# Leaving the order behind the attention to the scheduler, and issuing a batch's experts whole

## Chip, core and metric

The kernel runs on one core of one Trainium2 chip. The metric is the device time of one execution in microseconds (us), lower is better. A profiled execution of its own gives the span from the first to the last instruction and the trace.

## What is computed

One hybrid layer on x, of 4 batches x 1024 tokens x 128 features in fp32:

```python
x = x + softmax_attention(layernorm(x))        # 16 heads of 64, causal
x = x + experts(layernorm(x))                  # 32 experts 128x128, top 2 by softmax
x = x + linear_attention(layernorm(x))         # 16 heads of 8, cumulative sums over tokens
x = x + experts(layernorm(x))                  # the same experts again
```

`experts` multiplies each token with its two best experts' matrices, weighted with the softmax values. The linear attention forms `kv_cum = cumsum(k[:, :, None] * v[:, None, :])` over the tokens of a batch and divides `q . kv_cum` by `q . cumsum(k)`; the cumulative sums start anew with each batch.

## The kernel before

The tokens are held in SBUF in one tile, `x_sb`, as 32 tiles of 128 tokens, 8 to a batch. The kernel has three stages.

**Attention** (to L837) goes over 4 batches x 8 pairs of heads. The first `experts` of batches 0 to 2 are stepped beside it. It ends with the output projection of the last batch (`project_out`, L711 and L716), beside which the last gathers of batch 2 and the first statistics for the experts of batch 3 already run.

**Linear attention** goes over 32 steps u, one for each tile of 128 tokens. `prepare(t)` (L959 to L1034) makes the features of four tiles: statistics (L965), scaling (L980), transposes (L987), one product with all four weights (L998), four copies on ACT (L1002 to L1005), the bias on POOL (L1007), exponential, sigmoid and logarithm on ACT, and four sums on POOL (L1027, L1028). `products(u)` multiplies k and v into `kv` on POOL (L1048) and copies k on ACT (L1054). `cumulate(u)` adds kv to the running sums in PSUM with a triangular matrix on PE (L1066), `outputs(u)` multiplies them with q on DVE (L1086), `carry(u)` completes the sums for the next tile on PE (L1074), and `finish(u)` reduces, divides, transposes (L1107), projects (L1112) and adds to x_sb (L1115).

**Experts** (`experts`, L206 to L474) is a generator: each `yield` ends a step, and the caller decides what other work is issued between two steps. It has four parts:

1. Routing (L218 to L348): statistics, transposes and router products, softmax, top two, counts of tokens per expert (a matmul into `pc`, L290 and L294), and from the counts the row that each token has in a list sorted by experts. Work passes between DVE, POOL, ACT and PE some twenty times.
2. Scatter: 16 weighted tiles are made on ACT (L376) and written to `xs_d` in HBM by 16 indirect DMAs that POOL issues (L366), with a one-column memset (`between`, L370) behind each.
3. The loop over 47 blocks of 128 rows, in 12 groups: load of the rows (L402) and of the weights (L407; for the last 15 blocks SP loads the expert's number into a register, L411, and then issues a DMA of its own, L414), transposes (L433), copy (L435), products (L422), copy (L427), and store to `ys_d` (L428). All loads and stores stand in SP's queue.
4. Gather: 16 indirect DMAs on POOL (L441). For the first experts they add into x_sb; for the second ones (called with `came`) they land in tiles `y` that DVE adds (L468, L473), and the batch is written out (L474).

The second experts of batch 3 are done otherwise: `moe` (L850 to L928) multiplies its 8 tiles with all 32 experts: 128 matmul records at L900 (two to a matmul), whose results DVE (L915) and ACT (L908) weight and POOL sums (L922 to L924).

**The order.** From the attention's first instruction to the end of the linear attention, everything is within `order.enter_context(tc.manual_schedule())`: each engine takes its instructions in the order in which the program issues them, and that order is written out by hand. In the linear attention, `ahead(third)` is called three times a step; each call steps every running `prepare` once and then calls `beside()`, which pops one entry of `queue` (one scatter or one gather), starts a waiting batch's experts if its room is free, and steps each running `experts` once:

```python
        def beside():
            if queue:
                queue.pop(0)()
            while waiting and not rooms[(waiting[0] + 1) % 2].busy:
                b = waiting.pop(0)
                r = rooms[(b + 1) % 2]
                sides.append(experts(b, f"s{b}", banks, queue, r, came))
            for e in list(sides):
                if next(e, "end") == "end":
                    sides.remove(e)
```

So the first experts of batch 3 ("3") run beside the linear attention of batches 0 and 1, the second experts of batch b ("s0", "s1", "s2") are put on the waiting list at step u = 8b + 11, and what is left of s1 and s2 goes on beside `moe`, which lies behind `order.close()`.

PSUM tiles of the linear attention and of the experts come from one pool of four banks (`ps_l`, tag `ps1`); the running sums (`ps_c`) and the reduced outputs (`ps_n`) have banks of their own. The divided outputs `o` have three buffers, `m` two, `kv` three.

Of the kernel before, what the change touches and what calls it, by code (L numbers as in the profile page):

```python
# [20 lines left out]
def hybrid_kernel(  # L21
# [455 lines left out]
    order = ExitStack()  # L477
    order.enter_context(tc.manual_schedule())
    sides, queue = [], []
    banks = [None]  # L480
    with attn as ph:
# [253 lines left out]
        def beside(k):  # L735

            for _ in range(3 if k % 2 else 1):
# [5 lines that stand above are left out]
# [10 lines left out]
        def slot(u, two, k):  # L753
# [36 lines left out]
            next(outs, None)  # L790
            next(norms, None)
            beside(k)
            if u3 and u3.ib % 2:
                weighing.append(weigh(*units[-4][1]))
# [36 lines left out]
        for _ in project_out(*pend):  # L831
            if k == 1:
                assert not room.busy
                sides.append(experts(B - 1, f"{B - 1}", banks, queue, room))
                final = sides[-1]
            beside(k)
            k += 1  # L837

    late = ctx.enter_context(tc.tile_pool(name="late", bufs=1, reuse_waits="tile"))
    xp = ctx.enter_context(tc.tile_pool(name="xp", bufs=1, reuse_waits="tile"))
# [7 lines left out]
    def moe(nm_, store, first=0, beside=None, between=None):  # L850
        with ExitStack() as ph:
# [4 lines left out]
            for q in range(first, NT // 4):  # L856
                nm = f"{nm_}_{q}"
                c0 = q * 4
                if beside:
                    beside(q, ps_1)  # L860
# [175 lines left out]
    with lin as ph:  # L1036
# [86 lines left out]
# [5 lines that stand above are left out]
                b = waiting.pop(0)  # L1128
                r = rooms[(b + 1) % 2]
                sides.append(experts(b, f"s{b}", banks, queue, r, came))  # L1130
            for e in list(sides):
                if next(e, "end") == "end":
                    sides.remove(e)

        def ahead(third):

            nonlocal started
            while started < NT // G and 3 * G * started - AHEAD <= third:
                if G * started // NB == B - 1 and final in sides:
                    break  # L1140
                running.append(prepare(started, ps_1))
                started += 1
            for r in list(running):
                if next(r, "end") == "end":
                    running.remove(r)
            beside()

        for third in range(-AHEAD, 0):
            ahead(third)
        kv = products(0)  # L1150
        ends = []
        for u in range(NT + 4):
# [18 lines left out]
                ends.append(f)  # L1171
                kv = nkv
            ahead(3 * u + 2)
    order.close()

    def rest(pool):

# [40 lines left out]
```

## Time and profile before

| | before |
|---|---|
| median of 3 runs | 2079.35 us (2077.35 to 2085.32) |
| profiled execution, its own time | 2080.02 us |
| span of the profiled execution | 2078.1 us |
| granted TensorE clock, mean | 0.938 |
| last gather of the first experts of batch 2 issued (end of the attention's part) | 1502.4 us |
| first scatter of "3" / first load of its loop / its first gather | 1568.0 / 1617.0 / 1670.8 us |
| first scatter of s0 / first load of its loop / its first gather | 1782.7 / 1825.6 / 1896.5 us |
| last addition of the linear attention to x_sb (L1115) | 1891.3 us |
| last gather of s2 | 2049.7 us |

Busy time by stretches of the span, in us; the last two columns are the granted clock of TensorE and the mean busy share of the DMA engines:

| stretch | length | PE | DVE | ACT | POOL | clock | DMA |
|---|---|---|---|---|---|---|---|
| 0 to 1504, attention | 1504 | 1427.41 | 1069.24 | 979.81 | 830.54 | 0.99 | 0.12 |
| 1671 to 1727 | 56 | 38.42 | 32.03 | 26.57 | 47.23 | 0.85 | 0.15 |
| 1825 to 1892 | 67 | 49.87 | 36.45 | 19.40 | 33.04 | 0.75 | 0.53 |
| 1957 to 2028 | 71 | 54.57 | 35.01 | 18.20 | 27.72 | 0.78 | 0.60 |

An engine's row in the profile gives its line in the source, the engine, the operation, and "output<-inputs" by the program's names. SPq and POOLq are the queues of SP and of POOL: what they issue or wait for. Times in a timeline are a start and a duration, both in us; "[1.42 <-DVE m]" is idle time of the engine ahead of an instruction and what ended it. PE's durations are modelled.

### The profile page before, as it was taken

To read this page: it belongs to the slowest core of one execution; us is meant where nothing else is said; L and a number is where in the kernel's file an instruction comes from. 1 tells how busy PE (TensorE), PEld (TensorE's weight loads), DVE (VectorE), ACT (ScalarE), POOL (GpSimd) and SP (SyncE) were. 2 spreads that over 40 slices of the span, in tenths; PEclk is the share of its full clock that TensorE was granted. 3 is DMA by queue.
4 is the path that set the end of the run, shared out by engine and by line. 5 is a ranking of instruction groups with operands and counts; after the bars stand their busy time and mean duration, and the time that the engine had idled before them with its cause. 6 is when DMAs were issued, how large, how long until landed. Compare 5 with 4: busy or idle time off the path is not lost. (4 is left out here: it accounts for less than half of the span.)

```text
span 2078.1 us, 33646 instructions
## 1 busy us (share of the span) xinstructions
PE 1816.7 (87%) x10117; PEld 1056.7 (51%) x10117; DVE 1368.5 (66%) x3983; ACT 1200.5 (58%) x3721; POOL 1203.1 (58%) x2216
## 2 busy tenths in 40 slices
PE   5999999999999999999999999999547767774776
PEld 2555555555555655555565555556323534453442
DVE  4677776776887677678767777776326457653545
ACT  3766666676676566667756676676264444422322
POOL 3444444454675486466547645663748477966735
PEclk9999999999999999999999999999868988885877
DMA  7000000000003210000331000033300510054751
GB/s 209 1 1 1 1 1 1 1 1 1 1 16 102 83 17 5 1 1 12 91 95 19 8 1 1 12 87 98 67 0 18 163 33 7 20 162 124 205 152 37
DMA packets 173059, 96.56 MB, mean 46 GB/s; under 512 B 9264, under 2 KB 170064, under 8 KB 172752
## 3 DMA queue, kind: packets, MB, share of 16 engines
q1 hardware_dynamic: 158256, 78.16, 13.3%
q0 software_dynamic: 14336, 14.69, 3.3%
q8 instruction: 82, 1.34, 0.3%
q10 hardware_dynamic: 288, 1.57, 0.2%
q14 instruction: 97, 0.79, 0.1%
HBM read 57.23 MB, written 37.16 MB: 45 GB/s over the span
## 5 line engine op out<-in xcount | busy, mean ns | idle before, releaser
L599 DVE TENSOR_REDUCE nmx<-s 128x2 f32<-128x1024 f32 x512 | 604.2, 1219 | 217.5 <-PE s L590 207.2
L624 ACT ACTIVATE p<-s,nmx 128x512 f32<-128x512 f32 (+3 forms) x640 | 361.2, 575 | 316.3 <-DVE nmx L599 261.7
L590 PE MATMUL s<-kT,qT 64*128 64x512 f32 x2048 | 516.6, 618 | 8.5 <-ACT p L624 4.7
L666 POOL TENSOR_SCALAR p<-p,f,ri 128x512 f32<-128x512 f32 (+3 forms) x768 | 504.7, 675 | 0.7 <-DVE x_sb L716 0.2
L679 PEld LDWEIGHTS pt<-ident,p 128*128 128x128 f32 x2304 | 250.7, 141 | 218.8 <-issue 101.2
L679 PE MATMUL pt<-ident,p 128*128 128x128 f32 x2304 | 336.4, 282 | 25.3 <-ACT pT L683 7.6
L683 ACT COPY pT<-pt 128x512 f32<-128x512 f32 (+3 forms) x768 | 324.7, 509 | 14.9 <-PE pt L679 9.3
L648 POOL TENSOR_TENSOR rs<-rs,f 128x2 f32<-128x2 f32 x256 | 52.5, 205 | 428.0 <-ACT f L615 388.6
L696 PE MATMUL po<-pT,va 128*64 128x256 f32 (+1 forms) x2560 | 291.2, 365 | 0.6 <-DVE oT L703 0.6
L590 PEld LDWEIGHTS s<-kT,qT 64*128 64x128 f32 x2048 | 173.3, 185 | 194.6 <-issue 96.2
L629 ACT ACTIVATE p<-s,nmx 128x128 f32<-128x128 f32 x512 | 180.6, 366 | 103.4 <-DVE nmx L599 93.4
L696 PEld LDWEIGHTS po<-pT,va 128*64 128x64 f32 x2560 | 167.1, 136 | 97.2 <-issue 32.6
L644 POOL TENSOR_TENSOR rs<-rs 128x2 f32<-128x2 f32 x192 | 44.0, 229 | 193.7 <-DVE ri L657 193.7
L637 DVE SCALAR_TENSOR_TENSOR p<-p,qtri 128x128 f32<-128x128 f32 x512 | 145.3, 310 | 7.1 <-ACT p L629 4.0
L624 ACT ACTIVATION_READ_ACCUMULATOR p<-s,nmx 128x1 f32 x640 | 138.9, 217 | 0.0
L441 POOL DMA_INDIRECT x_sb<-ys_d,row x64 | 102.6, 1604 | 16.5 <-issue 16.4
L1066 PE MATMUL cum<-kv,tri 128*128 128x384 f32 x192 | 78.3, 549 | 27.0 <-POOL kv L1048 23.1
L716 DVE TENSOR_TENSOR x_sb<-pw,x_sb 128x128 f32<-128x128 f32 x128 | 36.9, 288 | 79.4 <-PE pw L711 78.2
L711 PE MATMUL pw<-wo_sb,oT 128*128 128x128 f32 x512 | 84.5, 290 | 0.7
L900 PE MATMUL pe_s<-we_sb,xnT_ms 128*128 128x512 f32 x128 | 75.0, 716 | 9.9 <-DVE x_sb L915 7.2
L711 PEld LDWEIGHTS pw<-wo_sb,oT 128*128 128x128 f32 x512 | 68.6, 190 | 27.9 <-ACT pT L683 12.7
L422 PE MATMUL pe_s<-we_s,xsT_s 128*128 128x128 f32 x282 | 53.3, 330 | 32.9 <-issue 19.1
(300 smaller groups left out, 2684.5 us busy)
## 6 DMA issues: line engine op xcount, KB each, us to landing
xs<-xs_d SPq DMA_DIRECT2D x44, 256.0 KB
ys_d<-ys SPq DMA_DIRECT2D x44, 256.0 KB
xs_s<-xs_d SPq DMA_DIRECT2D x33, 256.0 KB
ys_d<-ys_s SPq DMA_DIRECT2D x33, 256.0 KB
we<-_ffn_expert_weights_dram SPq DMA_DIRECT2D x32, 256.0 KB
we_s<-_ffn_expert_weights_dram SPq DMA_DIRECT2D x24, 256.0 KB
xs_d<-zero SPq DMA_DIRECT2D x2, 3008.0 KB
we<-_ffn_expert_weights_dram SPq DMA_DIRECT2D x60, 64.0 KB
```

The source lines that it names most:

```text
L441: g_.indirect_dma_start(to, None, yd, bass.IndirectOffsetOnAxis(ap=row[:, j, c : c + 1], axis=0), **how)
L590: nc.tensor.matmul(st[:, h, :], self.qT[rows, self.ib * P : (self.ib + 1) * P], self.kT[rows, j * 512 : (j + 1) * 512], start=True, stop=True,
L599: nc.vector.tensor_reduce(self.nmx[:, i, :], self.s[i], AX.X, ALU.max, negate=True)
L624: nc.scalar.activation(self.p[h][:, at : at + m * P], self.s[i][:, h, : m * P], AF.Exp, bias=bias, accum_out=self.rs[:, i, h : h + 1],)
L629: nc.scalar.activation(self.p[h][:, at + m * P : at + (m + 1) * P], self.s[i][:, h, m * P : (m + 1) * P], AF.Exp, bias=bias,)
L637: nc.vector.scalar_tensor_tensor(d, d, 1.0, qtri, ALU.mult, ALU.mult, accum_out=self.rs[:, 2, h : h + 1])
L666: nc.gpsimd.tensor_scalar(w, w, self.f[:, i, h : h + 1], self.ri[:, h : h + 1], ALU.mult, ALU.mult,)
L679: nc.tensor.transpose(pt[:, c * P : (c + 1) * P], self.p[h][:, (g + c) * P : (g + c + 1) * P], ident,)
L683: nc.scalar.copy(self.pTs[h][:, g : g + m, self.col : self.col + P], pt[:, : m * P].rearrange("p (c i) -> p c i", c=m),)
L696: nc.tensor.matmul(po[h * DH : (h + 1) * DH, c0:256], va[:, jb, h, :], pTs[h][:, jb, c0:], start=(jb == 0), stop=(jb == n - 1),)
L711: nc.tensor.matmul(pw[:, :P], oTs[i][:, c * P : (c + 1) * P], wo_sb[:, pr, :], start=(i == 0), stop=(i == len(prs) - 1),)
L1066: nc.tensor.matmul(sums[i][:, : EP * P], tri, part(kv, i), start=(u % NB == 0), stop=True, skip_group_check=True,)
```

## The change

Three things. The hand-written order ends with the attention (`order.close()` and a barrier that only the scheduler sees stand ahead of the `late` pools); what is issued behind it is put in order by the scheduler, engine by engine. When `beside()` starts a waiting batch's second experts, it steps them, and empties the queue, until nothing of them is left, so that all their instructions are issued ahead of the linear attention's later ones. And ahead of the first call of `ahead` the first experts of batch 3 are run to their end in the same way.

```diff
             beside(k)
             k += 1
 
+
+    order.close()
+    tc.no_sync_barrier()
 
 
     late = ctx.enter_context(tc.tile_pool(name="late", bufs=1, reuse_waits="tile"))
...
                 b = waiting.pop(0)
                 r = rooms[(b + 1) % 2]
                 sides.append(experts(b, f"s{b}", banks, queue, r, came))
+                while sides or queue:
+                    for e in list(sides):
+                        if next(e, "end") == "end":
+                            sides.remove(e)
+                    while queue:
+                        queue.pop(0)()
             for e in list(sides):
                 if next(e, "end") == "end":
                     sides.remove(e)
...
             beside()
 
+        while sides or queue:
+            beside()
         for third in range(-AHEAD, 0):
             ahead(third)
         kv = products(0)
...
             ahead(3 * u + 2)
-    order.close()
```

## Prediction

> **What bounds the kernel now.** I read the busy time by stretches first, then the rows of POOL and of SP's queue. The attention ends at 1503.5 us and the instruction lists of both builds are the same up to there, so the change can only touch the 575 us behind it. Columns: stretch, length, busy us (and instructions) of PE, weight loads, DVE, ACT, POOL; granted clock, DMA share, GB/s.
>
> ```profile
> 1504.00:1617.00 113.00, 63.10 (x167) 32.54 (x167) 49.26 (x134) 58.98 (x149) 77.56 (x109) 0.74 0.03 10
> 1617.00:1671.00 54.00, 43.72 (x219) 31.71 (x220) 27.38 (x57) 25.85 (x52) 20.60 (x17) 0.91 0.61 172
> 1727.00:1825.00 98.00, 72.07 (x212) 40.07 (x210) 68.28 (x188) 42.77 (x112) 84.09 (x103) 0.86 0.04 12
> 1892.00:1957.00 65.00, 34.75 (x151) 24.25 (x152) 24.23 (x76) 16.15 (x44) 52.13 (x81) 0.71 0.62 175
> 2028.00:2078.00 50.00, 32.78 (x55) 11.78 (x54) 26.64 (x86) 12.80 (x45) 30.16 (x32) 0.75 0.13 37
> ```
>
> From 1727 to 1825 POOL is busy 84 of 98 us: its queue, which holds kv products, routing and scatters, paces the linear attention. From 1892 on no engine is full; chains of transfers end the kernel. The hand order lays experts over linear attention: the loop of "3" (1617 to 1671) and that of s0 run while PE still does cumulative sums.
>
> Two waits matter:
>
> ```profile
> L441 POOLq EVENT_SEMAPHORE  x21: 17/43/5292, 1666.9 to 2035.3; - x21
> L441 POOL DMA_INDIRECT x_sb<-ys_d,row x16: 1540/1564/2392, 1670.8 to 1725.7; - x16
> L441 POOL DMA_INDIRECT y_s<-ys_d,row_s x48: 941/947/1447, 1896.5 to 2049.7; - x48
> ...
> 1664.62 3.39 SPq L428 DMA_DIRECT2D ys_d<-ys  x3
> ...
> 1668.09 2.15 POOL L1048 TENSOR_TENSOR kv<-kq,va 128x1024 f32<-128x1024 f32 x1
> 1670.79 1.68 POOL L441 DMA_INDIRECT x_sb<-ys_d,row  x1 [0.55 <-issue]
> ```
>
> A gather waits in POOL's own queue (up to 5.3 us) until the last store of the loop has landed (issued by 1668.0, gather at 1670.8). Whatever stands behind it on POOL waits too. Before, kv products and bias sums stand ahead of the first gather and between gathers.
>
> **What the change does to the lists.** On POOL, for each of the four batches, 16 gathers now follow 16 scatters with nothing between: POOL stands still for the whole loop. For "3", the first bias sum, ln sums and kv of the linear attention stand behind its gathers. On PE, nothing of the linear attention stands between a batch's first transpose `pxs` and its last group's products, since tiles of the shared PSUM pool are taken in program order; only sums already fed with kv run ahead, while routing goes on: PE's list has 17 steps u begun ahead of the loop of s0, 25 ahead of s1, all 32 ahead of s2. All matmuls of `moe` stand behind s2. So four holds, which lay under other work, now lie in a row with it.
>
> **The cost, stretch by stretch,** from 1503.5 us. Durations are those of rows of before.
>
> *Hold.* 16 scatters: 0.96 us and 0.3 to the next, 1.26 x 16 = 20.2. To the first load 1.5 (1615.6 to 1617.0). The loop took 53.8 (1617.0 to 1670.8); in its last four groups SP loads an expert's number before each DMA:
>
> ```profile
> 1644.68 3.77 SPq L414 DMA_DIRECT2D we<-_ffn_expert_weights_dram  x4
> 1648.56 0.38 SPq L428 DMA_DIRECT2D ys_d<-ys  x1
> ...
> 1650.58 3.76 SPq L414 DMA_DIRECT2D we<-_ffn_expert_weights_dram  x4
> ```
>
> These groups are 6 us apart, the eight earlier ones 3.2 (1617.0 to 1642.5). After, all 15 number loads stand ahead of the first row load, hidden under the scatters; if they cost their time elsewhere they give back up to 11 us. Four groups at 3.2 give 53.8 - 11 = 42.6. I take 47, between that and 53.8, since a loop alone keeps PE less busy and its clock lower. Gathers: 1.25 x 16 = 20 (second experts), 1.86 x 16 = 29.8 (first). A hold is 20.2 + 1.5 + 47 + 20 = 88.7; the first 98.5.
>
> *Routing of "3" alone.* POOL's last routing instruction ended at 1561.8, 58.3 us after the start; of these about 14 are linear attention's work on POOL that stood ahead (biases, scaling, four ln sums). 44, and 2 to the first scatter: 46. The 64 memsets (0.11 us each) move ahead of it into POOL's idle time; without that cover they cost 7.
>
> *Linear attention starts* when POOL is free: bias 1.27, ln sums 5.1, kv 2.15, and 3 for ACT's sigmoid and logarithm: 11.5. Its first projections lie under the gathers.
>
> *A step u.* With routing and scatters beside it, 9 steps in 80 us: 8.9. In the stretch with least interference,
>
> ```profile
> 1760.00:1780.00 20.00, 16.48 (x56) 9.07 (x55) 18.48 (x42) 12.08 (x35) 18.75 (x24) 1.00 0.00 0
> 1763.96 0.60 PE L987 MATMUL pxn_l<-ident,xn_l 128*128 128x128 f32 x4
> 1764.40 2.10 PE L1066 MATMUL cum<-kv,tri 128*128 128x384 f32 x6
> ...
> 1770.16 2.20 PE L1074 MATMUL cum<-kv,rest 128*128 128x384 f32 x6
> ```
>
> 3 steps in 20 us: 6.7. PE's rows add to 6.3 a step at full clock (2.1 + 2.1, projections 1.0, transposes and output 1.1). I take 7.2: no gathers or scatters on POOL, but some routing.
>
> *From the count matmul to the first scatter* POOL's row chain was 18 us (1543.6 to 1561.8) with 1.3 of bias in it; alone 15, and with three kv products (2.2 each) in between 22.
>
> Sum, each term a stretch on the path:
> - "3": 46 + 98.5 = 144.5, at 1648. Linear start 11.5: 1659.5.
> - s0: its count matmul stands behind 14.3 steps, 103; to scatter 22; hold 88.7: 1873.
> - s1: bias, ln sums and kv 9; 4.3 steps (u = 19 on) 31; 22; hold 88.7: 2024.
> - s2: 9; 3.9 steps 28; 15; hold 88.7: 2165.
> - `moe`: its rstd stands behind the last gather. Scaling, transposes, first products 11; 16 matmul records take 9.2 us at the end of before, 8 tiles 74, less 4 run ahead of the softmax: 70; last sums and store 8 (2066 to 2074). 89: 2254.
>
> The profiled execution's time is 1.9 above its span: **2256 us**, 8.4% slower; its own 2080.02 is within 0.03% of the median, so I forecast 2255 against that.
>
> Bounds: step 6.7 to 8.9 over 22.5 steps -11 to +36; loop 42.6 to 53.8, four times, -18 to +27; routing of "3" 42 to 58, -4 to +12; the three count-to-scatter chains 4 each, -12 to +12; `moe` 16 records at 9.2 to 11.5 (716 ns each, the mean of before), 0 to +18. The barrier adds no wait that the lists show: 0. The edges together are 2210 and 2360; all at one edge is unlikely.
>
> A rule that speaks against this change: the granted clock is 0.99 in the attention, 0.74 from 1504 to 1617, where PE is busy 63 of 113 us. The Trainium skill, "TensorE: Matmul & The Clock Gate", Part 1, says that TensorE falls to half clock after an idle window of some 3.4 us. If that held PE at half clock in all four loops, by an estimate 7 us longer each, the sum would be 2283; nothing above rests on it.
>
> **Rivals.**
> 1. *Every lone stretch is slower than its sum* (PE colder, gaps between engines not filled): step 8.9, loop 53.8, `moe` at 716 ns a record: 2255 + 36 + 27 + 18 = 2336. For it: 8.9 is what two long stretches show, clock 0.71 to 0.75 where PE has gaps. Against it: those had gathers on POOL and `moe` beside them.
> 2. *Gathers do not hold POOL.* If POOL passed its waits, the biases and kv would run under the loops: 16 saved at the start, 20 each at s0, s1, s2: 2179. Against it: the 5.3 us wait in POOL's queue.
> 3. *Linear attention runs under the holds after all* (the other side). Place: PE's queue during the loops. The steps and starts that I lay in a row are 103 + 31 + 28 + 11.5 + 18 = 191 us; under the holds they cost nothing, and the time is 2064, 0.8% faster. It decides from 175 of these 191 us on. For it: the first words of the change, a scheduler could fill gaps. Against: the lists have nothing to fill the loops with, and an engine's list is what it runs.
> 4. *The change does not move the order*: excluded by the lists but for a slip of mine; no change.
>
> **How the numbers follow.** Forecast (own range 2205 to 2310) 0.74; rival 1 0.18; rival 2 0.05; rival 3 0.02; rival 4 0.01. For 8 in 10 the range needs the forecast's cases and rival 1's nearer half, to 2340, and the bounds' low end with a little of rival 2: 2200 to 2345. Over 0.5% is about what a measurement of this kernel can tell from no change: slower 0.97, within 0.5% 0.01, faster 0.02.
>
> **What would show it.** Right: POOL idle for some 47 us ahead of the first gather of each of four batches, its wait ended by DMA stores of `ys`; no L1069 matmul (1066 before) between the first `pxs` and the last `pe` of a batch; first cumulative sum near 1660 (1565.8 before), first scatter of "3" near 1549, s0's first gather near 1853, s2's near 2145; number loads ahead of the row loads and groups 3 to 4 us apart to the loop's end; last 75 to 100 us nearly `moe` alone. Wrong: cumulative sums under a loop, POOL busy there, or a loop far from 47. The forecast falls most easily by the step: 1 us is 22.5.

## The result, and the profile after

The changed kernel takes 2243.81 us (median of 3 runs, 2234.62 to 2249.06) against 2079.35 before: a ratio of 1.0777, with a 95% interval of 1.0726 to 1.0828. The forecast was 2255 us, with a range of 2200 to 2345. The profiled execution of the changed kernel took 2243.81 us itself; its span is 2241.9 us, its mean granted clock 0.903 (0.938 before). The engines do the same work as before: PE is busy 1829.7 us in place of 1816.7, POOL 1201.2 in place of 1203.1. But for the 13 us on PE, the 164 us are idle time.

Line numbers of the linear attention and of `moe`'s products (L837 to L1130 before) are 3 higher in the changed kernel than in the kernel before. The busy time of the changed kernel by stretches (columns: stretch, length, busy us and instructions of PE, weight loads, DVE, ACT, POOL; granted clock, DMA share, GB/s):

```profile
1546.00:1567.00 21.00, 0.00 (x0) 0.00 (x0) 0.00 (x0) 5.08 (x15) 15.33 (x16) 0.50 0.15 50
1567.00:1612.00 45.00, 31.69 (x153) 24.89 (x154) 8.17 (x12) 11.21 (x27) 0.17 (x1) 0.71 0.73 206
...
1800.00:1843.00 43.00, 29.45 (x173) 23.16 (x174) 15.16 (x35) 14.06 (x38) 0.21 (x1) 0.86 0.77 216
...
1949.00:1996.00 47.00, 35.43 (x169) 28.56 (x169) 14.63 (x33) 12.10 (x34) 0.00 (x0) 0.68 0.70 198
...
2095.00:2143.00 48.00, 36.12 (x156) 30.56 (x156) 12.08 (x26) 8.02 (x17) 0.00 (x0) 0.57 0.60 171
2143.00:2163.00 20.00, 2.07 (x5) 1.18 (x5) 5.93 (x22) 0.51 (x2) 14.84 (x16) 0.50 0.17 49
2163.00:2242.00 79.00, 65.59 (x152) 28.98 (x152) 57.32 (x215) 29.02 (x100) 32.31 (x35) 0.89 0.05 15
```

The first row is the issue of 16 scatters: no matmul and no DVE work in 21 us. The rows of 43 to 48 us are the four loops: POOL does nothing in them but the first gather at the edge of two. In the last row but one 16 gathers are issued, and the last row is `moe` alone. That POOL waits, and for how long, stands ahead of the first gather of each batch (start, duration, instruction, idle time before it and what ended it; "issue" means that the profile found no event):

```profile
1611.83 1.62 POOL L441 DMA_INDIRECT x_sb<-ys_d,row  x1 [45.93 <-DMA we_s<-_ffn_expert_weights_dram]
```
```profile
1842.79 1.00 POOL L441 DMA_INDIRECT y_s<-ys_d,row_s  x1 [43.94 <-DMA ys_d<-ys_s]
```
```profile
1996.95 1.00 POOL L441 DMA_INDIRECT y_s<-ys_d,row_s  x1 [49.17 <-issue]
```
```profile
2143.59 0.99 POOL L441 DMA_INDIRECT y_s<-ys_d,row_s  x1 [50.12 <-DMA ys_d<-ys_s]
```

Before, the first gather of "3" stood behind a kv product and had waited 0.55 us. Now the four waits add to 189 us. The name of the releaser is right twice; for "3" the profile names a weight load that landed at the same moment, although the last store of `ys` had been issued 4.8 us earlier. And what of the linear attention ran meanwhile? The matmuls of L1069, its cumulative sums, by stretches (busy us and instructions of PE and weight loads, clock, DMA share, GB/s):

```profile
1567.00:1612.00 45.00, 0.00 (x0) 0.00 (x0) 0.71 0.73 206
1651.00:1779.00 128.00, 43.49 (x102) 21.59 (x102) 0.82 0.00 0
1800.00:1843.00 43.00, 0.00 (x0) 0.00 (x0) 0.86 0.77 216
...
1949.00:1996.00 47.00, 0.00 (x0) 0.00 (x0) 0.68 0.70 198
...
2095.00:2143.00 48.00, 0.00 (x0) 0.00 (x0) 0.57 0.60 171
```

None in a loop, and 102 records, which is 17 steps u of 6 records, between the gathers of "3" and the scatters of s0. Not all of the linear attention stands still, though: at a loop's end, among the last group's products and behind them, PE does 4 to 10 us of its other matmuls (projections and outputs, L990, L1001, L1110, L1115, and in the loops of s0 and s1 a few of `carry`, L1077).

### The profile page after: what moved, and what is told of

Its sections match the earlier page's. It is cut to its first block, busy times and chain, and to the rows that moved or that the text cites. A ratio compares the mean times of both kernels' runs of the same rounds, so it can differ in the third digit from the quotient of the medians.

```text
span 2241.9 us, 33697 instructions
## 1 busy us (share of the span) xinstructions
PE 1829.7 (82%) x10117; PEld 1072.3 (48%) x10117; DVE 1376.5 (61%) x3983; ACT 1203.5 (54%) x3720; POOL 1201.2 (54%) x2216
## 4 chain that ended last, share of the span: by engine, by line
PE 58%; POOL 11%; ACT 9%; DVE 9%; issue 9%; DMA 3%; SPq 1%; ACTq 0%; POOLq 0%; DVEq 0%
PE s L590 18%; PE pt L679 10%; PE po L696 9%; DVE nmx L599 5%; ACT p L624 3%; PE pw L711 3%; POOL x_sb L441 3%; PE pk L539 2%; PE pe_s L903 2%; PE pe_s L422 2%; PE pe L422 2%; ACT pT L683 2%; PE pv L553 2%; PE pq L545 1%; POOL kv L1051 1%
## 5 line engine op out<-in xcount | busy, mean ns | idle before, releaser
L679 PE MATMUL pt<-ident,p 128*128 128x128 f32 x2304 | 336.5, 282 | 25.3 <-ACT pT L683 7.6
L441 POOL DMA_INDIRECT x_sb<-ys_d,row x64 | 100.9, 1576 | 62.6 <-DMA we_s<-_ffn_expert_weights_dram 45.9
L441 POOL DMA_INDIRECT y_s<-ys_d,row_s x48 | 46.9, 977 | 157.0 <-DMA ys_d<-ys_s 94.1
L427 DVE COPY ys_s<-pe_s 128x512 f32<-128x512 f32 (+1 forms) x36 | 24.5, 680 | 158.2 <-PE pe_s L422 120.3
L1077 PE MATMUL cum<-kv,rest 128*128 128x384 f32 x168 | 79.8, 597 | 38.4 <-DVE m L1089 36.2
L1069 PE MATMUL cum<-kv,tri 128*128 128x384 f32 x192 | 81.0, 552 | 34.8 <-POOL kv L1051 30.8
L433 PE MATMUL pxs_s<-ident,xs_s 128*128 128x128 f32 x141 | 32.9, 369 | 92.0 <-DMA xs_s<-xs_d 92.0
L1051 POOL TENSOR_TENSOR kv<-kq,va 128x1024 f32<-128x1024 f32 x32 | 69.9, 2221 | 38.8 <-PE cum L1077 38.7
```

Of the source, the lines that this page charges most:

```text
L441: g_.indirect_dma_start(to, None, yd, bass.IndirectOffsetOnAxis(ap=row[:, j, c : c + 1], axis=0), **how)
L679: nc.tensor.transpose(pt[:, c * P : (c + 1) * P], self.p[h][:, (g + c) * P : (g + c + 1) * P], ident,)
L1051: nc.gpsimd.tensor_tensor(kv[:, :LD], k.rearrange("p (h d) -> p h d", h=LH).unsqueeze(1).to_broadcast([P, LD, LH, LD]), va[:, u % G, :].re ...
```

## The experiments

The theory, H: four holds (scatters, loop, gathers) stand one behind the other with the linear attention and `moe`, because a batch issued whole leaves nothing on POOL behind its gathers and nothing on PE between its blocks. The rivals: S, the scheduler's order itself costs the time; P, POOL's queue alone makes the hold; and, for the length of a loop, a cold TensorE against the transfers. The kernel before ran at 2070 to 2074 us beside these runs and at 2079 beside the first result, so I compare ratios to before; 1% is 20.7 us.

| kernel | median us | ratio to before, interval |
|---|---|---|
| the changed kernel | 2243.81 | 1.0777 (1.0726 to 1.0828) |
| e1 scheduler only | 2056.70 | 0.9940 (0.9923 to 0.9957) |
| e2 whole issue only, by hand | 2349.85 | 1.1342 (1.1321 to 1.1364) |
| e3 PSUM banks two and two | 2119.72 | 1.0238 (1.0214 to 1.0261) |
| e4 only "3" whole | 2108.53 | 1.0171 (1.0144 to 1.0198) |
| e5 only s0, s1, s2 whole | 2181.80 | 1.0553 (1.0520 to 1.0585) |
| e6 no second blocks | 2172.56 | 1.0480 (1.0458 to 1.0503) |
| e7 warm scatters | 2235.47 | 1.0774 (1.0737 to 1.0810) |
| e8 scheduler only, banks two and two | 2045.69 | 0.9882 (0.9866 to 0.9899) |
| e9 transposes first | 2215.06 | 1.0695 (1.0677 to 1.0712) |
| e10 e8 with transposes first | 2046.40 | 0.9883 (0.9867 to 0.9900) |
| e11 before, numbers early | 2052.12 | 0.9907 (0.9891 to 0.9924) |
| e12 e11 with transposes first | 2056.72 | 0.9917 (0.9903 to 0.9931) |

**e1: the scheduler without whole issue.** Against the changed kernel:

```diff
-                while sides or queue:
-                    for e in list(sides):
-                        if next(e, "end") == "end":
-                            sides.remove(e)
-                    while queue:
-                        queue.pop(0)()
...
-        while sides or queue:
-            beside()
```

> Only the first part of the change: the hand order ends behind the attention and the scheduler orders the rest; neither whole issue is there, so experts are issued by the step as before. Theory H (the loss is four holds in a row, made by the whole issue: a batch's gathers close POOL and its blocks close PE's list for the whole loop): without whole issue kv products stand between the gathers again and expert blocks between other matmuls, so the loops are hidden again; within 40 us of the kernel before, 2040 to 2120 us. Rival S (the loss is the scheduler's own order, whoever issues whole): most of the 164 us stay, 2180 us or more.

Measured: 0.994, that is 12 us faster than before. H holds and S falls: the scheduler does not cost the time, it gains a little. The group of gathers shows why (busy us and mean ns, then idle time before them and its main releaser). The changed kernel:

```profile
L441 POOL DMA_INDIRECT x_sb<-ys_d,row x64 | 100.9, 1576 | 62.6 <-DMA we_s<-_ffn_expert_weights_dram 45.9
L441 POOL DMA_INDIRECT y_s<-ys_d,row_s x48 | 46.9, 977 | 157.0 <-DMA ys_d<-ys_s 94.1
```

The kernel of e1:

```profile
L441 POOL DMA_INDIRECT x_sb<-ys_d,row x64 | 102.2, 1596 | 16.5 <-issue 16.2
L441 POOL DMA_INDIRECT y_s<-ys_d,row_s x48 | 46.5, 970 | 39.1 <-DVE x_sb L918 25.6 <-issue 11.3 <-DMA we_s<-_ffn_expert_weights_dram 1.9
```

The second row in the kernel before:

```profile
L441 POOL DMA_INDIRECT y_s<-ys_d,row_s x48 | 46.8, 976 | 33.3 <-DVE x_sb L915 19.7 <-issue 13.2 <-DMA we_s<-_ffn_expert_weights_dram 0.4
```

The wait of 46 us ahead of the gathers of "3" is gone; what is left of the first row, 16.2 of 16.5 us, is the 0.3 us from one issue to the next. The second row is back near that of before; its one long wait (25.3 us, at 2004.6) lies in s2 beside `moe`, as the 19.7 us did.

**e2: whole issue without the scheduler.** `order.close()` stands behind the linear attention again and the barrier is gone; both whole issues stay:

```diff
-    order.close()
-    tc.no_sync_barrier()
...
             ahead(3 * u + 2)
+    order.close()
```

> Only the other parts: both whole issues, but the order by hand holds to the end of the linear attention as before. Theory H: the four holds are there and cannot be helped; at least as slow as the changed kernel, and slower by what the scheduler repaired: number loads back between the row loads (up to 11 us a loop, 44) and routing of s0, s1, s2 with no linear attention issued beside it (58 us a batch from before's first batch, of which 15 to 22 were counted: some 30 each, 90). 2290 to 2380 us. Rival S (the scheduler's order is what costs): near the kernel before, 2040 to 2120 us.

Measured: 1.1342, 2349.85 us, inside H's range. The four waits ahead of the first gathers are 55.6, 55.7, 51.8 and 55.1 us in its trace, together 29 us more than in the changed kernel, and number loads stand between the row loads again (groups 5.8 us apart at the end of s0's loop, 1841.9 to 1859.2). The other 88 us (5.65% is 117) I put down to routing that has no linear attention issued beside it: for s0, 35 us pass on POOL from the first routing instruction (1757.2) to the first scatter (1792.4) without one kv product. That this makes up all of the 88 us is not shown. So the whole issue makes the loss, and the scheduler repairs a part of it.

**e4 and e5: one half of the whole issue each.** e4 has the first part of e1's diff (the inner `while` of `beside` goes), e5 the second (the two lines ahead of `for third in range(-AHEAD, 0)` go).

> The changed kernel without the whole issue of s0, s1 and s2; only batch 3 is issued whole, ahead of the linear attention. Theory H: of the four holds only the first is left. First cumulative sum at 1651 as in the changed kernel (1566 before), and from there the linear attention, 32 steps of 7.2 to 7.5 us, ends near 1885; the experts of s1 and s2 lie beside moe as before. The first hold costs 85 us of start less the 9 steps that before did meanwhile at 8.9 and now does at 7.3: 2079 + 20 to + 90, 2100 to 2170 us. Rival S: 2200 us or more.

> The changed kernel without the whole issue of batch 3 ahead of the linear attention; s0, s1 and s2 are still issued whole. Theory H (holds add up, each is paid once on the path): the scheduler alone took 2057 us, the first hold alone 2109, so the first is worth 52 and all four 187 over the scheduler alone; without the first 2244 - 52 = 2192, range 2175 to 2210 us, with the three holds of some 89 us seen as before. Rival (the first hold only moved a wait: without it the linear attention starts earlier and waits at s0 instead): 2225 to 2250 us.

Measured: 1.0171 (48 us over e1) and 1.0553 (127 us over e1); together 175 us, where the changed kernel has 173 over e1. The holds add up: 48 us for the first and 42 for each later one. Seen from the other end, e5 is 46 us faster than the changed kernel by the ratios, about what the first hold alone had cost. The wait of e4:

```profile
1613.51 1.63 POOL L441 DMA_INDIRECT x_sb<-ys_d,row  x1 [49.48 <-DMA we_s<-_ffn_expert_weights_dram]
```

It is e4's only long one; its 48 later gathers idle 14.2 us in all. In e5 there are three, 45.6, 46.6 and 40.7 us, ahead of s0, s1 and s2, and none ahead of "3".

**e3: the shared PSUM pool.** What keeps the linear attention off PE in a loop? The change to the changed kernel:

```diff
-        ps_1 = ph.enter_context(tc.tile_pool(name="ps_l", bufs=4, space=PSUM, reuse_waits="tile"))
+        ps_1 = ph.enter_context(tc.tile_pool(name="ps_l", bufs=2, space=PSUM, reuse_waits="tile"))
+        ps_x = ph.enter_context(tc.tile_pool(name="ps_x", bufs=2, space=PSUM, reuse_waits="tile"))
...
-        banks[0] = ps_1
+        banks[0] = ps_x
```

> The changed kernel, with the four shared PSUM banks split: two for the experts' tiles, two for the linear attention's. Precedence and whole issue stay. Theory H with the shared pool as PE's lock: cumulative sums now stand between a batch's transposes and products (the list shows them), so some 5 or 6 steps of 7.2 us run under the loop of 3, 4 or 5 under those of s0 and s1, and the start of the linear attention (9.5 us) under the first; s2's hold stays, as no linear attention is left. 14 to 16 steps, 100 to 115 us, and the start: 2120 to 2150 us. Rival P (POOL's queue alone holds, the pool is not the lock): kv products still come only behind the gathers, 2225 to 2250 us. Rival B (two banks are too few for either side and pace both): 2250 us or more.

Measured: 1.0238, 112 us faster than the changed kernel, with whole issue and precedence still there. Rivals P and B fall. Cumulative sums in the four loops of e3 (they are L1070 there; columns as above):

```profile
1567.00:1613.00 46.00, 10.29 (x22) 4.80 (x22) 0.81 0.57 165
1751.00:1796.00 45.00, 7.97 (x16) 3.52 (x16) 0.77 0.53 152
1885.00:1933.00 48.00, 11.22 (x24) 4.77 (x24) 0.86 0.68 195
1995.00:2043.00 48.00, 0.00 (x0) 0.00 (x0) 0.73 0.62 177
```

62 records in the first three loops, 10.3 steps; none in s2's, where no linear attention is left, and where the hold of 43.65 us ahead of the first gather stays. I had expected 14 to 16 steps there. 10.3 steps of 7.5 us and the start of 9.5 make 87 of the 112 us. The stretches above have the length of the changed kernel's loops. Up to the first gathers of e3 (1622.5, 1806.4, 1930.8) there are 76 records, 12.7 steps, but its four loops take 14.5 us more in all (55.1, 55.4, 45.4 and 42.2 from the first row load to the first gather): 90 us by this count. The rest I don't have from the trace alone; the scheduler now also puts the gathers of the first three batches behind kv products on POOL, so that the 20 to 30 us of gathers no longer stand alone. That this is the rest is argued, not measured.

**e6: a shorter loop.** Four of twelve groups fewer; the kernel leaves out the second blocks of crowded experts, a part of the computation:

```diff
-        groups = [(g, min(4, NTILE - g)) for g in range(0, NTILE, 4)]
+        groups = [(g, min(4, NTILE - g)) for g in range(0, E, 4)]
```

> The changed kernel with a loop of 8 groups in place of 12: the 15 second blocks of crowded experts are left out (their rows of the result are zeros written once at the start), and so are their number loads. It leaves part of the computation out. Theory H (each loop stands on the path whole): four groups of 3.2 us, four times: 51 us less, 2185 to 2205 us. Rival (other waits of a hold, such as routing on DVE or ACT, would show as soon as the loop is shorter): less than 25 us, 2220 us or more.

Measured: 2.97% less than the changed kernel, 62 us, where 51 were expected. Not all of it lies in the four holds. The edit shortens the experts that run beside the attention too, and the last gather of batch 2 is issued at 1480.7 in e6, at 1503.5 in the changed kernel: 22.8 us. The waits ahead of the first gathers are 37.1, 29.6, 38.1 and 37.5 us, which is 8.8, 14.4, 11.1 and 12.6 less, 46.9 in all or 2.9 a group. With the 22.8 us this is 69.7 of the 70.9 us between the two traces. So the loops stand on the path whole, at about the 3.2 us a group that I had taken from the loop of "3" before. Why the loops differ, 42.6 to 48.7 us in the changed kernel, is what the next experiments look at.

**e7: a warm TensorE ahead of the loop.**

```diff
                     later(scatter, t, j, cc_)
+                    if nm[0] == "s" or nm == "3":
+                        pq = banks[0].tile([P, 512], F32, tag="ps1", name=f"warm_{nm}_{cc_}_{j}")
+                        for i in range(4):
+                            nc.tensor.matmul(
+                                pq[:, i * P : (i + 1) * P], t, onesq, start=True, stop=True
+                            )
```

> The changed kernel with 4 small matmuls more for each scatter, whose results nobody reads, so that TensorE is not idle while the scatters are issued ahead of a loop. The loops took 44.5, 42.6, 47 and 48.4 us at granted clocks of 0.71, 0.86, 0.68 and 0.57. If a cold TensorE makes a loop longer, all four come to some 42.6 us: 12 us less in all, 2228 to 2236 us, and the clock in the loops is over 0.85. If the loops are paced by their transfers (170 to 216 GB/s in them): 2240 to 2250 us whatever the clock.

Measured: 1.0774, no gain. (2235 us lies in the range given for shorter loops, but the kernel before ran 9 us faster beside this run than beside the first result; the ratios are equal.) The extra matmuls did what they were for, but it did not last. Scatters, first loads and loop of s2 in e7:

```profile
2064.00:2084.00 20.00, 16.80 (x128) 16.61 (x128) 0.84 (x2) 5.75 (x16) 15.19 (x17) 0.83 0.13 44
2084.00:2090.00 6.00, 0.00 (x0) 0.00 (x0) 0.00 (x0) 0.00 (x0) 1.91 (x2) 0.82 0.27 83
2090.00:2126.00 36.00, 28.13 (x115) 24.15 (x116) 6.22 (x9) 5.85 (x10) 0.00 (x0) 0.50 0.66 187
```

PE waits 6 us for the first rows, and the clock is back at 0.50 for the whole loop. All four loops begin at half clock: a transpose takes 265 to 272 ns there, 150 ns at full clock. Only the loop of "3" became shorter (its wait 41.5 us in place of 45.9), and only there the clock rose much earlier, 6 us behind the loop's first matmul in place of 17; those of s0, s1 and s2 did not (10, 25 us and never, 10, 28 and never in the changed kernel). So e7 does not keep a loop warm and does not decide between clock and transfers; its one shorter loop is the one that was cold for a shorter time.

**e9: transposes ahead of products.** In the changed kernel's loop of s2 TensorE's rows read like this:

```profile
2102.92 2.08 PE L422 MATMUL pe_s<-we_s,xsT_s 128*128 128x128 f32 x8 [0.68 <-ACT xsT_s L435]
2104.79 1.06 PE L433 MATMUL pxs_s<-ident,xs_s 128*128 128x128 f32 x4
2106.58 2.08 PE L422 MATMUL pe_s<-we_s,xsT_s 128*128 128x128 f32 x8 [0.73 <-ACT xsT_s L435]
```

A group every 3.66 us: 2.93 of PE, then 0.73 of waiting for ACT's copy of the transposes. In the loop of s0 the same wait stands between the groups, but from 1812 on the clock is up:

```profile
1814.45 1.16 PE L422 MATMUL pe_s<-we_s,xsT_s 128*128 128x128 f32 x8 [0.73 <-ACT xsT_s L435]
1815.44 0.60 PE L433 MATMUL pxs_s<-ident,xs_s 128*128 128x128 f32 x4
```

The edit moves one block of the loop ahead of another:

```diff
+            if 0 <= i - 2 < len(groups):
+                g, n = groups[i - 2]
+                pt = banks[0].tile([P, 512], F32, tag="ps1", name=f"pxs_{nm}_{g}")
...
             if 0 <= i - 3:
                 g, n = groups[i - 3]
                 pe = banks[0].tile([P, 512], F32, tag="ps1", name=f"pe_{nm}_{g}")
...
-            if 0 <= i - 2 < len(groups):
-                g, n = groups[i - 2]
-                pt = banks[0].tile([P, 512], F32, tag="ps1", name=f"pxs_{nm}_{g}")
```

> The changed kernel with two blocks of the loop exchanged: a group's transposes are issued ahead of the products of the group before it, so that TensorE does not wait for ACT's copy of the transposes. In the loop of s2 in the changed kernel a group takes 3.66 us, 2.93 of TensorE at a granted clock of 0.50 and 0.73 of waiting for that copy. If this gap is what keeps the clock at half there (e7 showed that warming TensorE ahead of the loop does not hold), the clock rises within the first groups and the four loops come to 40 to 43 us: 12 to 18 us less, a ratio to before of 1.069 to 1.072 (the changed kernel 1.078). If the transfers pace the loop, or the clock stays at half all the same: 0 to 5 us less, 1.075 to 1.078.

Measured: 1.0695, 17 us faster than the changed kernel. The waits ahead of the first gathers are 40.4, 42.4, 42.2 and 42.5 us: 5.5, 1.5, 7.0 and 7.6 less. The loop of s2 in e9:

```profile
2083.04 2.06 PE L429 MATMUL pe_s<-we_s,xsT_s 128*128 128x128 f32 x8
2084.89 1.06 PE L422 MATMUL pxs_s<-ident,xs_s 128*128 128x128 f32 x4
2085.74 1.21 PE L429 MATMUL pe_s<-we_s,xsT_s 128*128 128x128 f32 x8
2086.79 0.60 PE L422 MATMUL pxs_s<-ident,xs_s 128*128 128x128 f32 x4
```

No wait, and from 2086 on the same instructions take half the time. In all four loops of e9 the clock is up 3 to 6 us behind the first matmul. In the changed kernel this took 10 us for s0, 17 for "3", 28 for s1, and for s2 the loop was nearly over; in the same order the loops took 42.6, 44.5, 47.8 and 48.7 us, with the same instructions and the same wait in each. The clock of three of them by stretches of 4 us ("3", s0, s1; columns as above):

```profile
1587.00:1591.00 4.00, 2.92 (x24) 2.44 (x23) 1.38 (x2) 0.85 (x2) 0.00 (x0) 1.00 0.96 269
1812.00:1816.00 4.00, 3.14 (x24) 2.72 (x24) 1.05 (x2) 0.66 (x2) 0.00 (x0) 1.00 0.91 252
1981.00:1985.00 4.00, 2.57 (x20) 2.34 (x21) 0.95 (x2) 1.17 (x2) 0.00 (x0) 1.00 0.86 242
```

So a TensorE that stays cold did cost up to 6 us a loop (s2 against s0), and e9 takes it away. The 0.73 us alone cost little where the clock is up: e9 gains 1.5 us in s0's loop. Nor do they fix the clock, since three loops warmed with them; without them all four did, and soon. What decides when the clock rises in a loop with this wait is open. With a warm TensorE a loop's wait ends at 40 to 42 us, with 262 GB/s in its middle: the next bound is the transfers, or something that moves with them.

**e8, e10, e11, e12: is there a kernel faster than both?** e8 is e1 with e3's banks; e10 is e8 with e9's order of the blocks; e11 is the kernel before with the expert numbers loaded ahead of the loop; e12 is e11 with e9's order.

```diff
+        nos = [
+            nc.sync.value_load(which[0:1, k : k + 1], min_val=0, max_val=E - 1)
+            for k in range(OVF)
+        ]
         room.busy = False
...
-                    e = nc.sync.value_load(
-                        which[0:1, k - E : k - E + 1], min_val=0, max_val=E - 1
-                    )
+                    e = nos[k - E]
```

> The first run's kernel (scheduler alone, 2057 us) with the PSUM banks split two and two. If tiles of the shared pool, taken in program order, still hold blocks and linear attention apart there: 10 to 30 us less, 2027 to 2047 us. If issue by the step already mixes them, as the list of TensorE says (cumulative sums between the blocks in both), two banks a side are only fewer: 2055 to 2085 us.

> The kernel of e8 (scheduler alone, PSUM banks two and two; 0.988 of before) with the same exchange of transposes and products. If TensorE's wait for the copy matters where blocks lie among other matmuls too, the loops of s1 and s2, which nothing covers at the end, become 3 to 8 us shorter each: 0.982 to 0.986 of before. If other matmuls fill that wait already, 0.986 to 0.990.

> The kernel before, its order by hand throughout, with one edit: SP loads the 15 expert numbers ahead of the loop, where its queue is free, and not between the row loads. The prediction set up to 11 us a loop on these loads (groups 6 us apart, 3.2 without). If that is their price, the loops of s1 and s2, which end the kernel before, become up to 11 us shorter each: 10 to 22 us less, 0.989 to 0.995. If the loads only fill waits for the groups' own transfers: 0.997 to 1.003.

> The kernel of e11 (order by hand, expert numbers loaded early, 0.991 of before) with the exchange of transposes and products of e9. If the loops of s1 and s2 at the end of the kernel by hand run on a TensorE at half clock too, as in the changed kernel, they become 3 to 7 us shorter each: 0.983 to 0.988 of before, level with the scheduler and two pools (0.988) or ahead of it. If other matmuls already fill the wait there, as e10 showed for the scheduler's order: 0.989 to 0.992.

Measured: e8 0.9882, with e10 the fastest of all, 12 us ahead of e1: two banks a side suffice. That they part what the shared pool had tied even without whole issue is the reason expected, not one that I followed in the trace. e10 0.9883, e12 0.9917: the order of the blocks gains nothing here; that other matmuls fill the wait already was expected and is not shown. In both, the exchange also reaches the experts beside the attention, whose last gather is issued at 1504.8 and 1505.1, in e8 and e11 at 1501.5 and 1501.4. e11 0.9907, 19 us: in the trace before, the last groups of s2's loop issue their weights at 1997.4, 2004.6, 2010.5 and 2015.6 (6.1 apart), in e11 at 1981.6, 1985.2, 1988.4 and 1992.1 (3.5 apart). Four groups at 2.6 us less are 10.4, what the prediction had set on a loop's number loads; they were a loss of the kernel before. The whole loop of s2, from its first row load to its last store, shrank by more, from 66.7 to 46.4 us; what else became shorter there is not settled. Nor is s2 all of it: in e11's trace s0's first scatter is 5.5 us earlier than before (1777.2), its first gather 20.0 (1876.5) and s2's last gather 28.1 (2021.6), so that more than half of the lead is there when s0's loop ends.

## Why the prediction was right

The forecast's mechanism and its size were right; term by term, measured in the changed kernel's trace:

| term | predicted us | measured us |
|---|---|---|
| "3": end of attention to first scatter | 46 | 42.3 |
| "3": scatters, loop and gathers | 98.5 | 95.5 |
| start of the linear attention | 11.5 | 9.5 |
| first cumulative sum to s0's count matmul (14.3 steps) | 103 | 107.8 |
| s0: count to scatter; hold | 22; 88.7 | 20.1; 84.2 |
| s0's gathers to s1's count matmul | 40 | 46.1 |
| s1: count to scatter; hold | 22; 88.7 | 18.7; 90.0 |
| s1's gathers to s2's count matmul | 37 | 41.0 |
| s2: count to scatter; hold | 15; 88.7 | 14.7; 90.0 |
| `moe` alone | 89 | 78.5 |

- *Hold.* Scatters and gathers came as their rows said (1.26 and 1.25 or 1.86 us each). The loops, from the first row load to the first gather, took 44.5, 42.6, 47.8 and 48.7 us: 45.9 in the mean, where I took 47. The reason given for taking more than 42.6, a lower clock in a lone loop, is what the four loops and e9 show.
- *PE's list.* "Nothing of the linear attention stands between a batch's first transpose and its last group's products, since tiles of the shared PSUM pool are taken in program order": the counts of L1069 show the first half for the cumulative sums, e3 the second. Taken at its word the first half is a little too strong: among the products of a last group stand some transposes and projections (L990, L1110, L1115; from 1834.2 on in the loop of s0). 17 steps ran ahead of s0, as the list had it.
- *POOL's queue.* Gathers held it 43.9 to 50.1 us. That is rival 2 gone.
- *A step u.* 7.2 was taken; 107.8 us for 14.3 steps is 7.5, and with the starts of 9 us kept, the two later stretches give 8.6 and 8.2. The clock was 0.82, 0.80 and 0.77 in them. These three terms were 15 us too small. (The upper bound of the step was too low by a slip: 8.9 less 7.2 over 22.5 steps is 38 us, not 36; nothing turned on it.)
- *`moe`.* Too large by 10.5: 5.1 us from the last gather to the first product in place of 11, and 65.4 us for 128 matmul records, 8.2 for 16 in place of 9.2. The end was 8, as predicted. This term and the steps nearly cancel, so part of the forecast's closeness is luck; all rows of the table together come to 12 us less than predicted.
- *Rival 1*, every lone stretch slow, was half there: the clock did fall to 0.57 to 0.86 in the loops, but no loop reached 53.8 and no stretch had steps of 8.9.
- *Rival 3*, linear attention under the holds, was wrong for this kernel, but its place was well chosen: PE's queue during the loops is what e3 opens, and it is worth 112 us.
- *The rule on the clock.* The Trainium skill, "TensorE: Matmul & The Clock Gate", Part 1, says that full clock comes after some 3.4 us of sustained work and is lost after an idle window of that length. The trace agrees where PE stood still (6 us in e7: 0.82 to 0.50). It goes beyond the rule in the loops: in that of s2 the clock stayed at 0.50 with no wait over 0.73 us, and in those of s0, "3" and s1 it rose with the same waits. The gain of e9, up to 7.6 us a loop, is the size that the prediction had named, 7 us, without giving its working. That estimate had been set on top of a loop of 47 us, though, which already held most of it.

What stays open: the 22 to 25 us of e3 that steps and start do not account for; what decides when the clock rises in a lone loop; and why e1 is 12 us faster than before. In its list all 15 number loads of "3" and s0 stand ahead of their loops, and e11 shows that such loads matter; but for s1 and s2 they stand between the row loads there as before.

## What to carry to other kernels

Before issuing a stage whole, look at what then stands behind its last wait on each in-order queue: a stage hidden under other work costs nothing until its own wait shuts that work out, and then the length of that wait is paid, once for each time it is issued (here 42 to 48 us a hold, with loops of 42.6 to 48.7). A scheduler can fill a stall only with work that its resources leave free; a pool of PSUM tiles shared by two streams and handed out in program order ties them together, and giving each its own two banks was worth 112 us in the changed kernel and 12 in the best one. And a short wait that returns in every turn of a loop should be read with the clock beside it: four loops with the same wait differed by 6 us, by how long they ran at half clock.

## What the runs showed of the hardware

- TensorE's granted clock can stay at 0.50 for over 30 us although PE is busy 82% of the time and waits no longer than 0.73 us in every 3.66 (changed kernel, loop of s2). The same wait did not keep it there in the loops of s0, "3" and s1, where it rose after 10, 17 and 28 us and was 1.00 with that wait still in the groups. The rows are those of s2:

```profile
2103.00:2115.00 12.00, 9.81 (x41) 8.61 (x42) 2.08 (x3) 1.76 (x3) 0.00 (x0) 0.50 0.75 214
2115.00:2131.00 16.00, 13.08 (x56) 11.48 (x56) 2.77 (x4) 2.34 (x4) 0.00 (x0) 0.50 0.72 201
```

- With that wait gone (e9) the clock rose within 6 us of the loop's first matmul in all four loops, and PE then needed far less time. In s2's loop it fell again near the loop's end with no wait of PE longer than 1.9 us in its rows, after PE had been busy 1.65 of 4 us:

```profile
2084.00:2088.00 4.00, 4.00 (x29) 4.00 (x28) 1.38 (x2) 1.10 (x2) 0.00 (x0) 0.74 0.78 226
2088.00:2104.00 16.00, 9.74 (x75) 8.27 (x73) 4.52 (x7) 3.58 (x7) 0.00 (x0) 1.00 0.93 262
2104.00:2108.00 4.00, 1.65 (x13) 1.42 (x13) 1.01 (x2) 0.58 (x1) 0.00 (x0) 0.82 0.87 247
2108.00:2112.00 4.00, 2.83 (x12) 2.57 (x13) 0.69 (x1) 0.48 (x1) 0.00 (x0) 0.50 0.62 172
```

- SP's loads of an expert number into a register go with some 0.65 us each where they stand between the DMA issues of its queue: groups of four were 6.1 us apart with them and 3.5 without (s2's loop, before and e11), and four DMA issues took 3.77 us with them and 1.97 without (loop of "3", before and changed kernel).
